# Layer 0 of a two-layer attention kernel: another order of the filler units, the row sums and the normalisation

## The chip, the cores and the metric

The kernel runs on one core of a Trainium2 chip. The metric is the device time of one execution in microseconds (us). Before the change three runs gave a median of 2808.86 us, the lowest 2808.78 and the highest 2810.7. Everything is fp32.

A core has a matrix engine (TensorE, "PE" in the profile, with its weight loads shown apart as "PEld"), a vector engine (VectorE, "DVE"), an engine for functions such as the exponential (ScalarE, "ACT"), a general engine (GpSimd, "POOL") and SyncE ("SP"), which here only issues transfers. Each engine runs its own instructions in its own order and waits at semaphores for the others. Matrix products land in PSUM, which has few buffers; all else lies in SBUF.

## The reference, cut to what matters

The input x has two images of 512 channels and 64x32 = 2048 tokens. Layer 0 is softmax attention with 8 heads of 64. The queries and keys see 64 more channels, 32 that depend on the row (frequency) alone and 32 that depend on the column (time) alone.

```python
emb = get_embeddings(B, H, W, FREQ_DIM, TIME_DIM, dtype)   # (B, 64, H, W): freq[h] and time[w]
qk_hs = concatenate([hidden_states, emb], axis=1)           # reshaped to (B, S, 576)
q = qk_hs @ Wq;  k = qk_hs @ Wk;  v = v_hs @ Wv             # 8 heads of 64
attn = softmax(q @ k^T * scale)
o = (attn @ v) @ Wout + bout
x = o + hidden_states                                       # layer 0

t = tokens(x)
t = t + attention_1(layernorm(t))                           # layer 1: Nystrom attention
t = t + ffn_1(layernorm(t))                                 # weights from 4-bit codes (qidx, scales)
```

The change leaves layer 1 as it is. Of layer 1, only the first layer norm and the preparation of the 4-bit weights are computed while layer 0 runs.

## The kernel before, in words

Layer 0 makes eight passes: two images b times four pairs of heads hp. `attention0` is one pass. It goes over 4 blocks t of 512 tokens and, within a block, over 16 chunks c of 128 keys, two chunks (a *group*) at a time, so 8 groups for a block and 32 for a pass. In the text, (t, c) names a group by its block and its last chunk. For each group the program issues, in this order:

1. the scores of the group (L1040, four 64x64 matmuls for each chunk into a PSUM bank pair), and their exponentials on ScalarE (L1048) into `p_f`, of which there are six buffers, that is three groups;
2. the additions of `p_f` into `acc_f` on VectorE (L1058), which make the softmax denominators;
3. the values of the group before (L1070), into two PSUM banks over the whole block; at the end of a block they are added by ScalarE and VectorE (L1076, L1077);
4. some *filler units*, see below;
5. one step of the preparation of layer 1's weights (`feed_forward_map`, VectorE almost alone, L1135, L1136, L1141), called `beside`, in the groups 1, 3 and 5 of each 8;
6. if a block has just ended, its row sums (`sums`): a matmul with ones (rs_f, L1084), the reciprocal on VectorE (L1088) and the product with the output on GpSimd (L1089).

The filler units keep TensorE busy and prepare the next pass. `Heads0.units` of the next pass gives 15: the query embedding (matmul L863 into fp, copy L865 to the factors `ft`, addition of the row and the column factor to a 128x2048 tile `e` on GpSimd, L867), four query projections (L879, a bank pp, with the addition of `e` on VectorE, L882), the same for the keys, four value projections (vp, L924), and a reduction of the largest entries (L912). Where an image is complete, `finish0_units` joins them: for each block the output projection in four units (yp, L939, with bias and x added on VectorE, L946; the sum x1 is written to DRAM by GpSimd's queue, L982) and the layer norm in steps (`statistics` and `norm0_steps`: L957 to L974, L991 to L995).

Units are Python generators. `advance(gens, n)` takes the first generator that can go on and draws units from it until n are made; a generator that yields GAP steps aside for the next one. How many are drawn in a group follows from `due`, the share of units that should be done by then. In most passes two units are drawn once two are due. While an image is being finished (`every`), one or two units are drawn in each group, and the weight preparation rests.

All of fp, pp, vp, yp, the row sums, and the mean and variance banks take turns in two PSUM buffers (`bank`).

At the start of the kernel, the units of the first pass run with nothing beside them: x, Wq and the embedding arrive, then the queries, keys and values of the first two heads are projected.

Of the kernel before, what the change touches and what calls it, by code (L numbers as in the profile page):

```python
# [19 lines left out]
KC = C // P  # L20
HEADS, D = 8, 64
NPAIR = HEADS // 2
TB = 512
# [638 lines left out]
def fast_path(  # L662
# [62 lines left out]
    def chunked(ap):  # L725
        return ap.rearrange("(k p) n -> p k n", p=P)
# [74 lines left out]


    emb_sb = wpool0.tile([64, H + W], F32, name="emb_f")
    nc.vector.memset(emb_sb, 0.0)
    w_sb = {kind: wpool0.tile([P, KC, C], F32, name=f"w{kind}_f") for kind in "qk"}
    we = {kind: wpool0.tile([64, C], F32, name=f"we{kind}_f") for kind in "qk"}

    def load_w0(kind, cols, queue=nc.sync):
        w = {"q": wq0, "k": wk0}[kind]
        nc.sync.dma_start(w_sb[kind][:, :, cols], chunked(w[:C, cols]))  # L810
        queue.dma_start(we[kind][:, cols], w[C:, cols])

    nc.gpsimd.dma_start(emb_sb[:32, :H], freq)
    nc.gpsimd.dma_start(emb_sb[32:, H:], time)
    load_w0("q", slice(0, P), nc.scalar)

    def load_x(src, b, name, first=0, n=NTB):
        tiles = []
# [21 lines left out]
    class Heads0:  # L840
# [13 lines left out]
        def embedded_and_projected(self, kind):  # L854

            cols, xbs = self.cols, self.xbs
            if kind == "q":
                self.q = qopool.tile([P, S], F32, tag="qo", name=f"q_{self.name}")

            def embedded(kind):  # L860

                fp = bank(f"fp_{kind}_{self.name}")
                nc.tensor.matmul(fp[:, : H + W], lhsT=we[kind][:, cols], rhs=emb_sb, start=True, stop=True)  # L863
                ft = wpool0.tile([P, H + W], F32, tag="ft", name=f"ft_{kind}_{self.name}", bufs=2)
                nc.vector.tensor_copy(ft, fp[:, : H + W])  # L865
                e = wpool0.tile([P, H, W], F32, tag="e", name=f"e_{kind}_{self.name}")
                nc.gpsimd.tensor_tensor(  # L867
                    e,
                    ft[:, :H].unsqueeze(2).to_broadcast([P, H, W]),
                    ft[:, H:].unsqueeze(1).to_broadcast([P, H, W]),  # L870
                    ALU.add,
                )
                return e.rearrange("p h w -> p (h w)")

            def project(kind, dst, e, t):
                toks = slice(t * TB, (t + 1) * TB)
                pp = bank(f"pp_{kind}_{self.name}_{t}")
                for k in range(KC):
                    nc.tensor.matmul(  # L879
                        pp, lhsT=w_sb[kind][:, k, cols], rhs=xbs[t][:, k, :], start=k == 0, stop=k == KC - 1  # L880
                    )
                nc.vector.tensor_tensor(dst[:, toks], pp, e[:, toks], ALU.add)  # L882

            dst = self.q if kind == "q" else self.k
            e = embedded(kind)
            yield
            yield GAP
            for t in range(NTB):
                project(kind, dst, e, t)
                yield  # L890
# [104 lines left out]
        nc.gpsimd.dma_start(chunked(xh_d[b])[:, :, toks], xn)  # L995
        yield

    N_FINISH0 = NTB * (KC + 2)

    def finish0_units(b, oTs, outs_done):  # L1000
        last = None
        for t in range(NTB):
            xb = block_of(lpool, "xr", f"xr_f0_{b}_{t}")
            nc.sync.dma_start(xb, chunked(x[b])[:, :, t * TB : (t + 1) * TB])
            yield from gap()

            for m, _ in enumerate(out0_units(b, t, xb, oTs)):
                if last and m == 0:
                    next(last)
                yield  # L1010
            if t == NTB - 1:
                outs_done.append(True)
            if last:
                yield from gap()
            xn = block_of(lpool, "xn", f"xn_f0_{b}_{t}")
            last = norm0_steps(b, t, xb, xn, xn[:, :2, :])
            next(last)
            yield from gap(2)
            next(last)
            yield  # L1020
            yield from gap(2)
            next(last)
            yield from gap(2)
            next(last)
            yield
        next(last)

    def attention0(hd, filler, n_filler, needed, beside=None, every=False):


        steps = [(t, c) for t in range(NTB) for c in range(NST)]
        av, acc, first, late = None, None, None, None

        def scores(t, c):
            sc = scores_bank(f"sc_{hd.name}_{t}_{c}")
            for r in range(2):
                for h in range(2):
                    rows = slice(h * D, (h + 1) * D)
                    lo = c * P + r * D
                    nc.tensor.matmul(  # L1040
                        sc[r * D : (r + 1) * D, h, :],
                        lhsT=hd.k[rows, lo : lo + D],
                        rhs=hd.q[rows, t * TB : (t + 1) * TB],
                        start=True,
                        stop=True,
                    )
            p = exps(f"p_{hd.name}_{t}_{c}")
            nc.scalar.activation(p, sc, AF.Exp, scale=D**-0.5)  # L1048
            return p

        def add(step, p):
            nonlocal acc, first
            t, c = step
            if c == 0:
                first = p
                acc = apool.tile([P, 2, TB], F32, tag="acc", name=f"acc_{hd.name}_{t}")
            else:
                nc.vector.tensor_tensor(acc, first if c == 1 else acc, p, ALU.add)  # L1058

        def values(step, pp, its_acc):  # L1060

            nonlocal av, late
            t, c = step
            if c == 0:
                av = [values_bank(f"av_{hd.name}_{t}_{r}") for r in range(2)]
            for r in range(2):
                keys = slice(r * D, (r + 1) * D)
                for h in range(2):
                    half = slice(h * D, (h + 1) * D)
                    nc.tensor.matmul(  # L1070
                        av[r][half, :], lhsT=hd.v[keys, c, half], rhs=pp[keys, h, :],
                        start=c == 0, stop=c == NST - 1,
                    )
            if c == NST - 1:
                o = hd.q[:, t * TB : (t + 1) * TB]
                nc.scalar.copy(o, av[0])  # L1076
                nc.vector.tensor_tensor(o, av[1], o, ALU.add)  # L1077
                late = t, its_acc

        def sums(t, acc):  # L1080
            o = hd.q[:, t * TB : (t + 1) * TB]
            rs = bank(f"rs_{hd.name}_{t}")
            for h in range(2):
                nc.tensor.matmul(  # L1084
                    rs[h * D : (h + 1) * D, :], lhsT=ones, rhs=acc[:, h, :], start=True, stop=True
                )
            rinv = row_of(f"rinv_{hd.name}_{t}")
            nc.vector.reciprocal(rinv, rs)  # L1088
            nc.gpsimd.tensor_tensor(o, o, rinv, ALU.mult)  # L1089

        pending, done = [], 0
        for i in range(0, len(steps) + 1, GROUP):
            group = [(step, scores(*step)) for step in steps[i : i + GROUP]]
            for step, p in group:
                add(step, p)
            for step, p, its_acc in pending:
                values(step, p, its_acc)
            pending = [(step, p, acc) for step, p in group]
            due = n_filler * (i + GROUP) // len(steps)
            if every:  # L1100
                done += advance(filler, 2 if due - done >= 2 else 1)
            elif due - done >= 2:
                done += advance(filler, min(due - done, 3))
            if beside and i // GROUP % 8 in (1, 3, 5):
                advance(beside)
            if not group:
                while needed in filler:
                    advance(filler)
            if late:
                sums(*late)  # L1110
                late = None

    def feed_forward_map():

# [559 lines left out]
    cur = Heads0(0, 0, xbs)  # L1674
    drain(cur.units())
    ffn_map = [feed_forward_map()]
    oTs, finish, work = [], None, []
    for n, (b, hp) in enumerate(todo[:-1]):
        nb, nhp = todo[n + 1]
        if nb != b:  # L1680
# [5 lines left out]
        else:  # L1686

            units = nxt.units(False, lambda: outs_done)
            work.append(finish)
            n_fill += N_FINISH0  # L1690
        work.append(units)
        attention0(cur, work, n_fill, units, ffn_map if finish is None else None, finish is not None)
        finish = None
        oTs.append(cur.q)
        if n == 3:
            while ffn_map:
# [3 lines left out]
        if hp == NPAIR - 1:  # L1700
            outs_done = []
            finish = finish0_units(b, oTs, outs_done)
            oTs = []
        cur = nxt
    only0.close()


# [407 lines left out]
```

## Time and profile before

| what | value |
|---|---|
| median of three runs | 2808.86 us |
| the profiled execution, its own time | 2808.29 us |
| its span in the profile | 2806.2 us |
| matmuls busy | 2745.0 us, 98% |
| VectorE busy | 1778.3 us, 63% |
| ScalarE busy | 913.5 us, 33% |
| GpSimd busy | 231.7 us, 8% |
| scores of layer 0 (L1040), busy | 491.7 us, 4096 matmuls |
| values of layer 0 (L1070), busy | 484.3 us, 4096 matmuls |
| query projections of layer 0 (L879) | 117.5 us, 256 matmuls |
| output projections of layer 0 (L939) | 115.9 us, 256 matmuls |
| row-sum reciprocals (L1088) | 107.2 us, 32, 3350 ns each |

The profiled execution took 0.6 us less than the median, and 2.1 us of it lie outside the span. In the rows of groups, the numbers after the bar are the busy time in us, the mean duration of one instruction in ns, and then the idle time of that engine just before, with what ended most of it. An fp32 matmul leaves two records in the timeline, each with its own start. Starts are exact, ends of pipelined matmuls are modelled, so the time from start to start is what a matmul costs when the engine is busy.

### The profile page before, as it was taken

What the parts mean: (1) busy time and instruction counts of PE and PEld (TensorE: products, weight loads), DVE (VectorE), ACT (ScalarE), POOL (GpSimd) and SP (SyncE); (2) the same over time, 40 slices, a digit from 0 to 9 for tenths busy, and PEclk for the clock granted to TensorE, in tenths of its full rate; (3) what the DMA queues carried; (4) which work ended last, traced back from release to release, by engine and by line L of the source; (5) the groups of instructions that cost most, each with busy time, mean ns of one, the idle gap of its engine ahead of it and who ended that gap; (6) DMA issues with size and microseconds to landing.
All of it is one profiled execution on the core that took longest, in us unless ns stands there. A gap on an engine that the chain in (4) does not pass through costs nothing. (4 is left out here: it accounts for less than half of the span.)

```text
span 2806.2 us, 39647 instructions
## 1 busy us (share of the span) xinstructions
PE 2745.0 (98%) x16746; PEld 1374.3 (49%) x16746; DVE 1778.3 (63%) x2109; ACT 913.5 (33%) x1352; POOL 231.7 (8%) x130
## 2 busy tenths in 40 slices
PE   9999999999999999999999999999999999999899
PEld 5343443434343334343344455777667666554333
DVE  2868788784658775767767544545755655556565
ACT  1434343433334334434422223223332323222110
POOL 1101101010101210100002000000100100000000
PEclk9999999999999999999999999999999999999999
DMA  3000000101001200002025632203001102010201
GB/s 113 5 5 1 5 1 1 61 16 46 27 32 60 75 1 1 1 31 67 16 83 180 202 120 89 97 28 114 27 28 50 65 1 86 23 61 19 101 16 46
DMA packets 85626, 140.31 MB, mean 50 GB/s; under 512 B 7856, under 2 KB 42944, under 8 KB 82880
## 3 DMA queue, kind: packets, MB, share of 16 engines
q1 hardware_dynamic: 80944, 120.87, 12.8%
q0 software_dynamic: 4416, 16.79, 1.6%
q8 instruction: 133, 2.18, 0.3%
q14 instruction: 53, 0.43, 0.0%
q10 hardware_dynamic: 80, 0.03, 0.0%
HBM read 82.48 MB, written 55.19 MB: 49 GB/s over the span
## 5 line engine op out<-in xcount | busy, mean ns | idle before, releaser
L1058 DVE TENSOR_TENSOR acc_f<-acc_f,p_f 128x1024 f32<-128x1024 f32 x448 | 611.4, 1365 | 217.8 <-ACT p_f L1048 188.8
L1048 ACT ACTIVATE p_f<-sc_f 128x1024 f32<-128x1024 f32 x512 | 496.8, 1022 | 580.2 <-PE sc_f L1040 574.1
L1040 PE MATMUL sc_f<-q_f,k_f 64*64 64x512 f32 x4096 | 491.7, 595 | 2.9 <-ACT p_f L1048 2.9
L1070 PE MATMUL av_f<-p_f,v_f 64*64 64x512 f32 x4096 | 484.3, 589 | 0.0
L1070 PEld LDWEIGHTS av_f<-p_f,v_f 64*64 64x64 f32 x4096 | 156.5, 133 | 283.0 <-issue 283.0
L1040 PEld LDWEIGHTS sc_f<-q_f,k_f 64*64 64x64 f32 x4096 | 144.8, 133 | 293.8 <-issue 253.0
L1214 PE MATMUL pp<-xh,w 128*128 128x512 f32 x512 | 231.2, 604 | 4.6 <-ACT X L1261 3.9
L1214 PEld LDWEIGHTS pp<-xh,w 128*128 128x128 f32 x512 | 95.7, 192 | 125.8 <-issue 113.9
L1506 PE MATMUL pb<-R 128*128 128x192 f32 (+1 forms) x640 | 149.6, 380 | 1.0 <-DVE M L1519 1.0
L1506 PE MATMUL pa<-M 128*128 128x192 f32 (+1 forms) x640 | 150.6, 380 | 0.0
L1595 DVE RECIPROCAL acc<-acc 128x256 f32<-128x256 f32 x64 | 111.4, 1746 | 46.7 <-ACT acc L1590 46.7
L1089 POOL TENSOR_TENSOR q_f<-q_f,rinv_f 128x512 f32<-128x512 f32 x32 | 68.3, 2135 | 825.6 <-DVE rinv_f L1088 825.5
L1601 POOL TENSOR_TENSOR o<-o,acc 128x512 f32<-128x512 f32 x32 | 53.8, 1682 | 885.1 <-DVE acc L1600 778.1
L924 PE MATMUL vp<-w,xh 128*128 128x128 f32 x1024 | 122.3, 278 | 0.0
L924 PEld LDWEIGHTS vp<-w,xh 128*128 128x128 f32 x1024 | 118.6, 194 | 7.2 <-issue 4.2
L924 PEld LDWEIGHTS vp_f<-wv_f,x 128*128 128x128 f32 x1024 | 115.6, 192 | 12.7 <-issue 11.0
L879 PE MATMUL pp_q_f<-x,wq_f 128*128 128x512 f32 x256 | 117.5, 612 | 4.2 <-DVE q_f L882 3.1
L939 PE MATMUL yp_f<-q_f,wo_f 128*128 128x512 f32 x256 | 115.9, 606 | 4.2 <-DVE rinv_f L1088 3.3
L924 PE MATMUL vp_f<-wv_f,x 128*128 128x128 f32 x1024 | 118.5, 276 | 0.0
L1506 PEld LDWEIGHTS pb<-R 128*128 128x128 f32 x640 | 106.5, 190 | 24.4 <-DVE M L1519 2.1
L1506 PEld LDWEIGHTS pa<-M 128*128 128x128 f32 x640 | 108.2, 193 | 20.4 <-ACT M L1497 2.5
L1654 PE MATMUL fp_g<-xn_g,mT 128*128 128x512 f32 x256 | 115.1, 598 | 0.7 <-ACT p L1568 0.7
(202 smaller groups left out, 3009.6 us busy)
## 6 DMA issues: line engine op xcount, KB each, us to landing
xh<-xh_fd SPq DMA_DIRECT2D x12, 1024.0 KB, 5.4
xr_f<-in_x_dram SPq DMA_DIRECT2D x8, 1024.0 KB, 5.1
x_fd<-xr_f POOLq DMA_DIRECT2D x8, 1024.0 KB, 4.7
xh_fd<-xn_f POOLq DMA_DIRECT2D x8, 1024.0 KB, 4.6
k_fd<-k SPq DMA_DIRECT2D x32, 256.0 KB, 2.7
q_fd<-q SPq DMA_DIRECT2D x32, 256.0 KB, 3.0
xb_g<-x_fd SPq DMA_DIRECT2D x32, 256.0 KB, 4.5
k<-k_fd SPq DMA_DIRECT2D x8, 1024.0 KB, 5.9
```

What stands on the lines that cost most here:

```text
L879: nc.tensor.matmul(pp, lhsT=w_sb[kind][:, k, cols], rhs=xbs[t][:, k, :], start=k == 0, stop=k == KC - 1)
L924: nc.tensor.matmul(vp[:, j * P : (j + 1) * P], lhsT=xb[:, k, j * P : (j + 1) * P], rhs=w_of(k), start=k == 0, stop=k == KC - 1,)
L939: nc.tensor.matmul(yp, lhsT=wo_sb[:, k, m * P : (m + 1) * P], rhs=oTs[k][:, toks], start=k == 0, stop=k == NPAIR - 1,)
L1040: nc.tensor.matmul(sc[r * D : (r + 1) * D, h, :], lhsT=hd.k[rows, lo : lo + D], rhs=hd.q[rows, t * TB : (t + 1) * TB], start=True, stop=True,)
L1048: nc.scalar.activation(p, sc, AF.Exp, scale=D**-0.5)
L1058: nc.vector.tensor_tensor(acc, first if c == 1 else acc, p, ALU.add)
L1070: nc.tensor.matmul(av[r][half, :], lhsT=hd.v[keys, c, half], rhs=pp[keys, h, :], start=c == 0, stop=c == NST - 1,)
L1089: nc.gpsimd.tensor_tensor(o, o, rinv, ALU.mult)
L1214: nc.tensor.matmul(pp, lhsT=self.w[j][:, c, :], rhs=xhs[t][:, c, :], start=c == 0, stop=c == KC - 1)
L1506: nc.tensor.matmul(dst, lhsT=lhsT[:, k, t * P : (t + 1) * P], rhs=rhs[:, k, :], start=k == 0, stop=k == 1)
L1595: nc.vector.reciprocal(half, half)
L1654: nc.tensor.matmul(fp, lhsT=mT[:, k, m * P : (m + 1) * P], rhs=self.xn[:, k, :], start=k == 0, stop=k == KC - 1,)
```

## The change

It has five parts.

- **Order of finishing an image.** `finish0_units` now only does the output projections of all four blocks, with the next block's x loaded ahead into the other of two buffers, and writes x1 to DRAM. A new generator, `norm0_units`, waits until that is done, then reads x1 back from DRAM block by block and makes the normalisation in steps. It takes the place of `beside` in the passes of the second image.
- **Drawing of units.** `every` is gone. In all passes four units are drawn, once four are due. `beside` is advanced in every second group, not in three of eight.
- **Row sums.** `sums` of a block is called one group later than before, except at the end of a pass.
- **First embedding sums.** For the first pass alone, the two additions that make `e` are done by VectorE, not by GpSimd.
- **Queues at the start.** The two embedding loads move from GpSimd's queue to ScalarE's, behind the first slice of Wq, which moves there from SyncE's; the memset of the embedding tile is split in two halves, so that it does not overlap the loaded parts.

```diff
-    nc.vector.memset(emb_sb, 0.0)
+    nc.vector.memset(emb_sb[:32, H:], 0.0)
+    nc.vector.memset(emb_sb[32:, :H], 0.0)
...
     def load_w0(kind, cols, queue=nc.sync):
         w = {"q": wq0, "k": wk0}[kind]
-        nc.sync.dma_start(w_sb[kind][:, :, cols], chunked(w[:C, cols]))
+        queue.dma_start(w_sb[kind][:, :, cols], chunked(w[:C, cols]))
         queue.dma_start(we[kind][:, cols], w[C:, cols])
 
-    nc.gpsimd.dma_start(emb_sb[:32, :H], freq)
-    nc.gpsimd.dma_start(emb_sb[32:, H:], time)
     load_w0("q", slice(0, P), nc.scalar)
+    nc.scalar.dma_start(emb_sb[:32, :H], freq)
+    nc.scalar.dma_start(emb_sb[32:, H:], time)
...
-                nc.gpsimd.tensor_tensor(
+
+                engine = nc.gpsimd if self.b or self.hp else nc.vector
+                engine.tensor_tensor(
...
     def finish0_units(b, oTs, outs_done):
...
+        def load(t):
+            xb = block_of(lpool, ("xr", "xn")[t % 2], f"xr_f0_{b}_{t}")
+            nc.sync.dma_start(xb, chunked(x[b])[:, :, t * TB : (t + 1) * TB])
+            return xb
+
+        nxt = load(0)
+        yield from gap()
         for t in range(NTB):
...
+            xb = nxt
+            if t + 1 < NTB:
+                nxt = load(t + 1)
+            yield from out0_units(b, t, xb, oTs)
+        outs_done.append(True)
+
+    def norm0_units(b, outs_done):
+
+        while not outs_done:
+            yield
+        for t in range(NTB):
+            xb = block_of(lpool, "xr", f"x1_f0_{b}_{t}")
+            nc.sync.dma_start(xb, chunked(x1_d[b])[:, :, t * TB : (t + 1) * TB])
+            yield
+            xn = block_of(lpool, "xn", f"xn_f0_{b}_{t}")
+            for _ in norm0_steps(b, t, xb, xn, xn[:, :2, :]):
                 yield
...
-            if every:
-                done += advance(filler, 2 if due - done >= 2 else 1)
-            elif due - done >= 2:
-                done += advance(filler, min(due - done, 3))
-            if beside and i // GROUP % 8 in (1, 3, 5):
+            if due - done >= 4:
+                done += advance(filler, 4)
+            if beside and i // GROUP % 2:
                 advance(beside)
             if not group:
                 while needed in filler:
                     advance(filler)
-            if late:
-                sums(*late)
-                late = None
+                ended = late
+
+            if ended:
+                sums(*ended)
+            ended, late = late, None
...
-        attention0(cur, work, n_fill, units, ffn_map if finish is None else None, finish is not None)
+        attention0(cur, work, n_fill, units, norm if b else ffn_map)
...
             finish = finish0_units(b, oTs, outs_done)
+            next(finish)
+            norm.append(norm0_units(b, outs_done))
```

By the order of instructions, a pass that prepares weights now has the query embedding's factors at (1,1), the row sums of block 0 at (1,3), the four query projections at (1,5), the keys' factors at (2,7), the four key projections at (2,11) and the four values at (3,11). Before, they went in pairs at (0,9) to (3,11), and the row sums of block 0 stood at (1,1). The first pass of the second image has the output projections of the four blocks at (0,9), (1,1), (1,9) and (2,1).

## The prediction, made before the changed kernel was run

> **What bounds the kernel now.** I read the busy shares first, then the waits of TensorE, then the stages that those point to. The change touches layer 0 alone (up to about 1421 us of the span).
>
> ```profile
> span 2806.2 us, 39647 instructions
> PE 2745.0 (98%) x16746; PEld 1374.3 (49%) x16746; DVE 1778.3 (63%) x2109; ACT 913.5 (33%) x1352; POOL 231.7 (8%) x130
> ...
> L1058 DVE TENSOR_TENSOR acc_f<-acc_f,p_f 128x1024 f32<-128x1024 f32 x448 | 611.4, 1365 | 217.8 <-ACT p_f L1048 188.8
> ```
>
> TensorE is 98% busy, so a gain must come from its few waits or from busy time that isn't arithmetic. VectorE looks idle for a third of the time, but its sums line waits for the exponentials 188.8 of 217.8 idle us. It follows at short distance in the first five passes, where it also prepares the weights of layer 1.
>
> ```profile
> PE rs_f L1084 <- DVE acc_f L1058: 3.8, 4, 1.2
> PE yp_f L939 <- DVE rinv_f L1088: 3.3, 2, 2.4
> PE pp_q_f L879 <- DVE q_f L882: 3.1, 1, 3.1
> PE sc_f L1040 <- ACT p_f L1048: 2.9, 8, 0.9
> PE mean_n L961 <- DVE xn_f L958: 2.8, 1, 2.8
> ...
> PE var_n L974 <- DVE xr_f L971: 1.6, 1, 1.6
> ```
>
> Columns: us in all, times, longest. All are stalls in layer 0 by VectorE (one by ScalarE). The head, in windows (us; busy PE, PEld, DVE, ACT, POOL; clock):
>
> ```profile
> 16.00:19.40 3.40, 0.28 (x2) 0.04 (x1) 0.79 (x2) 0.00 (x0) 2.58 (x1) 1.00 1.09 356
> 19.40:28.20 8.80, 8.80 (x17) 3.58 (x17) 1.19 (x2) 0.00 (x0) 0.00 (x0) 0.81 0.81 230
> ```
>
> and in the timeline, with the place in the second pass where a first query projection is put among the attention:
>
> ```profile
> 14.96 3.62 POOL L867 TENSOR_TENSOR e_q_f<-ft_q_f 128x2048 f32<-128x2048 f32 x1 [11.54 <-issue]
> 19.36 8.83 PE L879 MATMUL pp_q_f<-x,wq_f 128*128 128x512 f32 x16 [3.12 <-DVE q_f L882]
> ...
> 239.74 1.90 PE L1070 MATMUL av_f<-p_f,v_f 64*64 64x512 f32 x16
> 241.56 7.13 PE L879 MATMUL pp_q_f<-x,wq_f 128*128 128x512 f32 x16
> 241.72 5.80 DVE L1058 TENSOR_TENSOR acc_f<-acc_f,p_f 128x1024 f32<-128x1024 f32 x2
> 241.93 4.51 POOL L867 TENSOR_TENSOR e_q_f<-ft_q_f 128x2048 f32<-128x2048 f32 x1 [13.51 <-DVE ft_q_f L865]
> 248.63 1.95 PE L1040 MATMUL sc_f<-q_f,k_f 64*64 64x512 f32 x16
> 249.56 2.55 DVE L1058 TENSOR_TENSOR acc_f<-acc_f,p_f 128x1024 f32<-128x1024 f32 x2
> 250.40 1.90 PE L1070 MATMUL av_f<-p_f,v_f 64*64 64x512 f32 x16
> 252.11 1.90 PE L1040 MATMUL sc_f<-q_f,k_f 64*64 64x512 f32 x16
> ```
>
> Two things to see. First, sixteen attention records take 252.11-250.40 = 1.71 us from start to start, but 241.56-239.74 = 1.82 before the projection and 250.40-248.63 = 1.77 after it, and the projection takes 7.07 for 6.86 (16 records of 0.429). So one **excursion** from 64x64 tiles to another form and back costs about 0.36 us (0.11+0.20+0.05). Second, a pair of sums takes 2.55 us, and 5.80 while GpSimd adds an embedding.
>
> [...] the trace has half-clock windows of 3.413 us starting at 20.44, 727.0 and 942.0, each soon after a stall of 2.4 to 3.1 us. [...] here one sum goes from 1.22 to about 4.5 us.
>
> **The change, part by part (time of TensorE, start to start).** Matched against ideal pitches, TensorE loses 31.8 us in layer 0, besides the drains.
>
> *Four units at once, projections first: excursions.* By the two programs' order on TensorE, layer 0 makes 105 excursions before and 73 after. 32 x 0.36 = **-11.5**. The matmuls are the same.
>
> *First embedding on VectorE, its loads on another queue: head.* The first query projection starts at 9.11 and its four units end at 28.12: 19.01 for 32 matmuls of two records, 32 x 0.429 = 13.73; 5.3 lost (3.1 wait, 2.2 half clock). GpSimd starts the embedding at 14.96 although the factors are ready at 9.47. On VectorE, with 2.28 us (the 128x2048 subtraction of L962), it is done at about 11.8. The x blocks land at 12.3, 15.0, 17.8, when they are needed or before; the ScalarE queue has no other work then. **-5.2**.
>
> *Row sums a group later.* The 32 rs_f matmuls wait 4.95 us by pitches for the last addition of VectorE (3.8 in the waits view, the rest are shorter). With 3.43 us more of scores and values before them nearly all goes: **-4.9**. Reciprocal and GpSimd product come later, and their result is read a pass later.
>
> *Output projections first, normalisation from DRAM.* The stretch 721 to 972 us loses 14.2 us: yp waits for the reciprocal and for additions, mean and var wait, and two half-clock windows of 1.7 us each. After, yp come by fours with x loaded ahead, norm steps lie 8.6 us or more apart (one each second group), so that each matmul finds its input: **-14.2**, and a 0.9 us wait at 564.7 goes: **-0.9**. The norm re-reads 4 x 1 MB from DRAM; the same transfer (in_x) lands in 5.1 us, and a step of 6.9 us lies between. On SP these four loads stand behind loads of x that don't wait; nothing urgent follows. Square root and the exponential's table (0.69 + 1.28 us) fit before the next exponential.
>
> Sum of gains: 11.5+5.2+4.9+14.2+0.9 = **36.7 us**.
>
> *What four units at once cost.* All these units use one PSUM tag of two buffers, shared with the row sums. Before, two units found both free. After, in a pass with weight preparation, the order is: factor fp_q in group (1,1) (block, last chunk), row sums 0 in (1,3), four query units in (1,5). The second unit takes the buffer of row sums 0, thus waits for the reciprocal (3.27 us pitch), which stands on VectorE behind all sums of (1,3). And VectorE does more: weight preparation steps (2.1 us: two hits pairs of 0.42+0.69) in 4 of 8 groups rather than 3.
>
> I made a ledger for the second pass, in us from its first score (217.96), VectorE's instructions by their own durations: first addition ends 9.4 (as now, behind a reciprocal of the pass before, 222.87 to 226.2), then sums end at (0,3) 12.8, (0,5) 17.5, (0,7) 20.0, (0,11) 27.1, (0,15) 34.2, each followed by 2.1 for a hits step every second group; (1,1) 37.5, output sum 0.6, factors 0.2; GpSimd's embedding then makes (1,3) end at 44.0 instead of 40.8; 1.3 for scales; reciprocal to 48.6. TensorE: scores of (1,3) at 30.3, row sums at 34.3, (1,5) at 35.3, the batch starts at 38.9; the first unit ends at 42.5, the second waits until 48.7: 6.2 lost. Its own eviction and the row sum add 0.6 and 0.35: **7.2 us**, and a half-clock window of 1.7.
>
> The same working gives 2.5 for the first pass, 6.6 for the third, 0 for the fourth (weight preparation has other steps there), 0 for the fifth, 4.3 for the sixth (mean 2.0 and its start 1.4), 2.8 for the seventh: 7.2+2.5+6.6+4.3+2.8 = **+23.4**; three half-clock windows **+5.1**. ScalarE's exponentials need the sums of three groups before (six p_f buffers); that bears a lag of some 9 us, which isn't reached. Bounds: if VectorE recovers some 6 us more than I reckon, 0 to 5; if each stall is 3 us longer, 45.
>
> Net -36.7+28.5 = -8.2: 2808.3-8.2 = 2800.1 against the profiled execution, which is 0.6 below the median and 2.1 above its span. Forecast 2800.
>
> **Rivals.**
> (B) *The stall of the batch doesn't come* because VectorE is close behind the exponentials at (1,3). For it: now it catches up in every block, and the sums take 1.22 us alone. Against it: the 5.80 pair. Then 2808.3-36.7+5 = 2777.
> (C) *Slower: VectorE also holds up the key batches.* At (2,11) four key units stand in one group, their embedding asked of GpSimd two groups before. By the ledger this batch has 0.8 us to spare. Every weight or norm step that VectorE does late, and every sum stretched to 4.5 us by GpSimd, goes into a wait of TensorE there and at (1,5). More than 13.8 us beyond my 28.5, 2.3 in each of six passes, makes the kernel measurably slower; at 3.2 in each it is 2808.3-36.7+28.5+19 = 2819. [...] Against: later passes have no weight preparation.
> (D) *The excursions are not the price of a change of tile form*, but of something that stays per unit: 2808.3-25.2+28.5 = 2811.6.
>
> **How the numbers follow.** 0.2% (5.6 us) is about what a measurement of this kernel can tell from no change: faster is below 2803.2, slower above 2814.5. The ledger (own range 2794 to 2806) has 0.48: 0.34 faster, 0.14 same. B 0.17: faster. C 0.25: 0.05 same, 0.20 slower. D 0.10: 0.02 faster, 0.06 same, 0.02 slower. In all 0.53, 0.25, 0.22. The range 2781 to 2817 leaves out about a tenth at each end: half of B below, the worse half of C above.
>
> **What would show it.** Right: TensorE's records dense from 9 to 28 us; no waits of rs_f for acc_f above 0.3; none of yp_f for rinv_f; a wait of pp_q_f for the reciprocal of about 6 us in the second and third pass; 73 excursions at 0.36. Wrong: pp_k_f waits of over 2 us in each pass (C); no pp_q_f wait (B); attention groups above 3.43 us without a wait named, or exponentials waiting for acc_f (then the lag is larger than the buffers bear); waits of mean or var for the re-read x1.

## The result and the profile after

The changed kernel takes 2827.02 us (median of four runs, 2825.05 to 2830.39) where the kernel before took 2808.82 (2808.51 to 2810.7) beside it: a ratio of 1.0068, 95% interval 1.0053 to 1.0083. It is 18.2 us slower, where 8.8 us less were forecast. The profiled execution has a span of 2826.5 us, 20.3 more than before.

The page of the changed kernel, with the lines that answer to those of before (lines from L867 on have moved by 2 or 3):

```profile
span 2826.5 us, 39665 instructions
## 1 busy us (share of the span) xinstructions
PE 2754.9 (97%) x16746; PEld 1380.4 (49%) x16746; DVE 1787.4 (63%) x2112; ACT 915.5 (32%) x1354; POOL 223.5 (8%) x126
...
L1060 DVE TENSOR_TENSOR acc_f<-acc_f,p_f 128x1024 f32<-128x1024 f32 x448 | 607.0, 1355 | 173.6 <-ACT p_f L1050 139.5
...
L1072 PE MATMUL av_f<-p_f,v_f 64*64 64x512 f32 x4096 | 499.8, 595 | 19.9 <-DVE q_f L1079 19.9
```

VectorE's sums take about the same time (607.0 us, 611.4 before), but they wait 139.5 us for the exponentials where they waited 188.8: VectorE is late more often. The last line is new. In the kernel before, the values waited for nothing at all (the last number below); now they wait 19.9 us.

```profile
L1070 PE MATMUL av_f<-p_f,v_f 64*64 64x512 f32 x4096 | 484.3, 589 | 0.0
```

The waits of TensorE in layer 0 after the change (us in all, times, longest), with those of layer 1 left out:

```profile
PE av_f L1072 <- DVE q_f L1079: 19.9, 6, 5.4
...
PE sc_f L1042 <- ACT p_f L1050: 4.9, 11, 0.9
...
PE pp_q_f L882 <- DVE rinv_f L1090: 1.1, 1, 1.1
```

The waits of the row sums for `acc_f` are gone, and of the 3.3 us that yp waited for the reciprocal 0.9 are left. The wait of 6 to 7 us that the prediction put at the query batch is only 1.1. One stands instead that it did not name: the first values of a block wait for L1079, VectorE's addition of the two `av` banks of the block before. Those two banks have one buffer each. The timeline of the second pass, at the start of its block 1:

```profile
245.10 5.21 DVE L1060 TENSOR_TENSOR acc_f<-acc_f,p_f 128x1024 f32<-128x1024 f32 x4
...
247.76 1.03 PE L1072 MATMUL av_f<-p_f,v_f 64*64 64x512 f32 x4
...
252.35 1.22 DVE L1060 TENSOR_TENSOR acc_f<-p_f,p_f 128x1024 f32<-128x1024 f32 x1
...
253.48 0.68 DVE L1079 TENSOR_TENSOR q_f<-av_f,q_f 128x512 f32<-128x512 f32 x1
...
254.22 3.68 PE L1072 MATMUL av_f<-p_f,v_f 64*64 64x512 f32 x12 [5.42 <-DVE q_f L1079]
```

At 247.76 TensorE begins the values of block 1: four records, which go to the bank that ScalarE has already copied. The other twelve wait for the end of L1079 at 254.16. VectorE is then still busy with sums of block 0, does a weight step (L1137, L1138) between 250.2 and 252.4 and then the first sum of block 1; L1079 stands behind them all. The same place in windows (columns as before; the clock is the third number from the end):

```profile
230.00:247.70 17.70, 17.70 (x166) 6.31 (x160) 16.78 (x19) 10.27 (x12) 0.00 (x0) 1.00 0.01 2
247.70:251.30 3.60, 1.09 (x8) 0.15 (x2) 3.41 (x5) 1.39 (x2) 0.00 (x0) 1.00 0.00 0
251.30:261.50 10.20, 7.28 (x26) 1.62 (x29) 10.06 (x17) 0.00 (x0) 4.48 (x1) 0.50 0.00 0
```

In the first window VectorE is busy 16.78 of 17.70 us: a long stretch of attention without a projection between. In the third the clock is 0.50 for 10.2 us, of which the first 2.9 still lie inside the wait: TensorE is busy 7.28 us there. In the kernel before, the records of a query projection start 0.429 us apart at 1.00 and 0.853 at 0.50 (24.16 to 27.60 us and 21.05 to 23.61), so half of the time at 0.50 is reckoned as lost. The stall thus costs twice: the wait of 5.42 us, and half of some 7.3 us. By the records of the clock layer 0 has 41.0 us at half clock after the change and 10.2 before. Half of that is 20.5 and 5.1 us; TensorE stood idle in 4.4 of the 41.0, so 18.3 are lost after the change.

Where the 20.3 us of span come from: apart from drains, TensorE loses 64.0 us in layer 0 by starts, 31.8 before, which is +32.2. The span without this loss is 2762.5 instead of 2774.4: -11.9, the excursions saved. The sum is +20.3. (Of the 11.9, 1.0 lies behind layer 0, which ends 21.2 us later than before; 10.9 are left for the excursions.) Of the 32.2, 12.0 are waits that the view names in layer 0 (32.0 against 20.0) and some 13 are half clock; the rest are losses by starts that no wait names.

### The profile page after: what moved, and what is told of

Its sections match the earlier page's. It is cut to its first block, busy times and chain, and to the rows that moved or that the text cites. A ratio compares the mean times of both kernels' runs of the same rounds, so it can differ in the third digit from the quotient of the medians.

```text
span 2826.5 us, 39665 instructions
## 1 busy us (share of the span) xinstructions
PE 2754.9 (97%) x16746; PEld 1380.4 (49%) x16746; DVE 1787.4 (63%) x2112; ACT 915.5 (32%) x1354; POOL 223.5 (8%) x126
## 3 DMA queue, kind: packets, MB, share of 16 engines
q0 software_dynamic: 4352, 16.78, 1.6%
## 5 line engine op out<-in xcount | busy, mean ns | idle before, releaser
L1060 DVE TENSOR_TENSOR acc_f<-acc_f,p_f 128x1024 f32<-128x1024 f32 x448 | 607.0, 1355 | 173.6 <-ACT p_f L1050 139.5
L1072 PE MATMUL av_f<-p_f,v_f 64*64 64x512 f32 x4096 | 499.8, 595 | 19.9 <-DVE q_f L1079 19.9
L942 PE MATMUL yp_g<-o,wo_f 128*128 128x512 f32 x256 | 114.5, 596 | 0.0
```

The source lines that it names most:

```text
L942: nc.tensor.matmul(yp, lhsT=wo_sb[:, k, m * P : (m + 1) * P], rhs=oTs[k][:, toks], start=k == 0, stop=k == NPAIR - 1,)
L1072: nc.tensor.matmul(av[r][half, :], lhsT=hd.v[keys, c, half], rhs=pp[keys, h, :], start=c == 0, stop=c == NST - 1,)
```

## The experiments

The theories, with letters of their own, apart from those of the prediction's rivals. A (block start): between batches of four, VectorE gets a dozen groups of attention in a row; it comes late to L1079, and the values wait. B: VectorE's load alone, a step in 4 groups of 8 rather than 3. C: the late row sums. E, added later: the batches of four by themselves. Each kernel was timed in five rounds beside the kernel before.

**One part undone at a time.** Two units drawn instead of four:

```diff
-            if due - done >= 4:
-                done += advance(filler, 4)
+            if due - done >= 2:
+                done += advance(filler, min(due - done, 3))
```

> The changed kernel, but two units are drawn once two are due, as before the change. Theory A (block start): the first values of a block wait for VectorE's addition of the block before (L1079), which empties the single PSUM bank av, because between batches of four units VectorE gets a dozen groups of attention in a row and falls behind; units in between give it time. Expects the waits of av_f for q_f to fall from 19.9 to under 4 us, half-clock time in layer 0 from 41 us (20.5 lost) to under 15, 94 instead of 73 excursions (21 x 0.36 = 7.6 us back): 2795 to 2806 us. Rival B (VectorE's load alone: a weight or norm step in 4 of 8 groups instead of 3): the waits stay over 12 us, 2818 us or more. Rival C (row sums a group later): waits and time about as in the changed kernel, 2827.

A step in three groups of eight:

```diff
-            if beside and i // GROUP % 2:
+            if beside and i // GROUP % 8 in (1, 3, 5):
```

> The changed kernel, but a weight or norm step only in groups 1, 3 and 5 of 8, as before the change. A step is 2.1 us of VectorE. Theory A: each block start comes 2.1 us less late; waits of av_f for q_f 8 to 14 us (from 19.9), 2810 to 2822 us. Rival B (the load of VectorE is the cause, the batches are harmless): the waits vanish (under 3 us), 2795 to 2803 us. Rival C: 2827.

The row sums at once:

```diff
-                ended = late
-            if ended:
-                sums(*ended)
-            ended, late = late, None
+            if late:
+                sums(*late)
+                late = None
```

> The changed kernel, but the row sums of a block are put in at once, not a group later. Theory A: the addition L1079 stands ahead of the reciprocal in both orders; TensorE now waits at the row sums (rs_f for acc_f, 8 us or more) for a part of what it waited for at av_f; the sum of both is as before, time within 6 us of 2827. Rival C (the late row sums are the cause): waits of av_f gone and no new ones, 2800 to 2812 us. Rival B: 2827.

Measured: two_units 2825.69 us (ratio to before 1.0066, 1.0052 to 1.0079), three_of_eight 2817.94 (1.0036, 1.0024 to 1.0048), sums_at_once 2810.15 (1.0006, 0.9998 to 1.0015). A's expectation holds for the second kernel alone. Undoing the batches brought 1.3 us, not 21 to 32, and the av waits were still 13.2 us, as B had it; but in the second kernel, where B expected waits under 3 us, they are 12.2. Undoing the row sums brought 16.9 us although A said it would bring at most 6; the time is C's, but not the waits, for rs_f now waits 13.4 us for `acc_f`. No theory of one cause stands. Therefore the parts were also undone in combination:

> The changed kernel with two units at once and a weight or norm step in 3 of 8 groups, both as before the change; row sums stay a group later. Theory A, widened by the runs so far (what counts is how late VectorE is when a block begins: steps, places of the units and order of the sums add up, and none alone explains it): VectorE is no later than in the kernel before, so the waits of av_f for q_f are under 4 us, half-clock loss in layer 0 under 7 us, and the gains of the other parts show: 2808.5-4.3 (head, as measured) -14 (finish) -3 (row sums) -5 (91 excursions against 105) = 2782; 2780 to 2792. Rival C (late row sums cost by themselves, since the values that wait stand before them): waits of av_f over 8 us, 2798 us or more.

> The changed kernel with a weight or norm step in 3 of 8 groups and the row sums at once, both as before the change; four units at once stay. The single edits gave 2817.9 and 2810.2 against 2827.0. Theory A: both shorten the same lateness, so the gains overlap in part: 2798 to 2806 us, waits of rs_f and av_f together 5 to 10 us. Rival B (steps and order are separate costs that add): 2827-9-17 = 2801 or less, waits under 4 us. Rival E (the batches of four are the cause by themselves): 2808 us or more.

> The changed kernel with two units at once, 3 of 8 steps and row sums at once, all as before the change: what stays of it is the order of finishing (projections first, norm from DRAM) and the start. Theory A: no lateness beyond that of the kernel before: 2808.5-4.3-14 = 2790; 2786 to 2796 us, 105 excursions, rs_f waits for acc_f again 3 to 6 us. If the new order of finishing costs by itself (the norm steps load VectorE in the sixth and seventh pass): 2797 us or more, with waits of av_f, rs_f or mean_n over 4 us there.

Together (medians; "4/8" is a step in four groups of eight; excursions by the order of the instructions; the last column is half of the time at half clock in layer 0, from the clock records, of which up to 2.2 us fell on an idle TensorE):

| parts of the change present | us | excursions | half of half clock, us |
|---|---|---|---|
| none of the three (all_three_back) | 2801.6 | 105 | 0 |
| late sums (two_and_three) | 2801.1 | 91 | 1.7 |
| four units (three_at_once) | 2807.9 | 76 | 11.9 |
| four units, 4/8 (sums_at_once) | 2810.2 | 72 | 13.7 |
| four units, late sums (three_of_eight) | 2817.9 | 77 | 10.2 |
| 4/8, late sums (two_units) | 2825.7 | 94 | 11.9 |
| all three (the changed kernel) | 2827.0 | 73 | 20.5 |

two_and_three has the small waits and the small clock loss that A expected, but its time is 9 us above A's range, and all_three_back is 6 us above, where the second reading in its expectation (the new finishing costs by itself, 2797 us or more) holds; the finishing, which both have, is taken up below. three_at_once is 2 us above A's range, with waits of rs_f for acc_f of 17.7 us, which is nearer to E. Read row by row: late sums alone cost nothing (-0.5). Four units alone cost 6.3, although 29 excursions of 0.36 us are saved. Late sums cost 10.0 on top of four units (known to some 4 us only, since the six runs of three_of_eight spread from 2812.3 to 2821.0), and 16.9 on top of four units and 4/8. 4/8 costs 24.6 on top of late sums, with no batches of four, and 2.3 with four units and the sums at once. What costs most is the late sums together with a late VectorE; the batches aren't needed for it.

One part alone in the kernel before:

```diff
-            if beside and i // GROUP % 8 in (1, 3, 5):
+            if beside and i // GROUP % 2:
```

> The kernel before with one part of the change alone: a weight step in 4 of 8 groups instead of 3 (its own row sums, units in pairs, finishing and start). Theory A: VectorE needs 2.55+1.05+0.4 us for a group of 3.43 and comes late at the block starts: rs_f waits for acc_f and av_f waits for q_f go from 3.8 to over 12 us, half clock follows, 2818 us or more. Rival E (only the batches of four make VectorE late): 2808 to 2812 us.

Measured 2811.73 (1.0015, 1.0009 to 1.0022): 4.1 us slower, not 10, and in the range of E, which two_units contradicts. This run and two_units have the same units at the same places in the first pass and the same load of VectorE; there they differ in the late sums, and in the start before the pass. The output sum of block 1 (L1079, L1077) begins 78.4 us after the first scores of the pass in the one and 78.3 in the other, so VectorE is equally late. It shows what the late sums do. The timelines at the start of block 2 of the first pass, first of two_units, then of before_four_of_eight, each with a window of the 6.8 us after it:

```profile
130.59 1.03 PE L1072 MATMUL av_f<-p_f,v_f 64*64 64x512 f32 x4
...
133.15 0.68 DVE L1079 TENSOR_TENSOR q_f<-av_f,q_f 128x512 f32<-128x512 f32 x1
...
133.89 2.83 PE L1072 MATMUL av_f<-p_f,v_f 64*64 64x512 f32 x10 [2.26 <-DVE q_f L1079]
```

```profile
133.90:140.70 6.80, 6.80 (x16) 2.27 (x17) 2.29 (x2) 0.00 (x0) 0.00 (x0) 0.50 0.01 2
```

```profile
132.33 1.08 PE L1084 MATMUL rs_f<-acc_f,ones 128*64 128x512 f32 x4 [0.97 <-DVE acc_f L1058]
...
133.34 1.95 PE L1040 MATMUL sc_f<-q_f,k_f 64*64 64x512 f32 x16
...
135.45 0.68 DVE L1077 TENSOR_TENSOR q_f<-av_f,q_f 128x512 f32<-128x512 f32 x1
```

```profile
136.20:143.00 6.80, 6.80 (x24) 2.79 (x25) 6.70 (x4) 0.23 (x1) 2.12 (x1) 1.00 0.01 2
```

With the row sums at once, TensorE waits 0.97 us for the last sum, does row sums and scores, and by then most of VectorE's lateness has passed; the values lose about 1.1 us more by starts. With late sums, the row sums stand behind the values that wait. All the lateness falls on one wait of 2.26 us, and behind it the clock is 0.50 for 6.8 us; in the other kernel it stays 1.00 (what decides this is taken up in the last section).

**The bank taken out.** ScalarE copies both banks, VectorE adds the copies:

```diff
                 nc.scalar.copy(o, av[0])
-                nc.vector.tensor_tensor(o, av[1], o, ALU.add)
+                half = apool.tile([P, TB], F32, tag="rinv", name=f"oh_{hd.name}_{t}")
+                nc.scalar.copy(half, av[1])
+                nc.vector.tensor_tensor(o, half, o, ALU.add)
```

> The changed kernel, but ScalarE copies both av banks to SBUF (0.59 us more a block), and VectorE adds the two copies there, so that TensorE's bank does not wait for VectorE. VectorE's work is the same. Theory A: the waits of av_f for q_f go (under 1 us for ScalarE's copy), 19.9 us and their half clock; but VectorE is as late as before, so the next wait is the one that the prediction named: the second of four query units waits for the reciprocal of the row sums, 6 to 7 us in the second and third pass and some 5 in the passes with norm steps: 2808 to 2822 us. Rival D (the lag itself isn't that large; only the single bank makes it cost): no new wait over 2 us, 2790 to 2800 us.

Measured 2815.77 (1.0025, 1.0015 to 1.0035). The waits view of act_copy has no line of av_f for q_f any more; it begins with

```profile
PE pp_q_f L882 <- DVE rinv_f L1092: 16.0, 5, 6.0
```

A's expectation holds in time, and nearly in waits. This is the wait that the prediction reckoned with, at the place and of the size it named (6.0 us the longest). It was hidden behind an earlier one: a VectorE that comes late is met first by the values, and when these have waited, the batch finds it in time.

**Start and finishing.** The kernel before with the new start alone (the edits to the loads, the memsets and the engine of `e`, as in the change):

> The kernel before with the start of the changed one alone: the first two embedding additions on VectorE and the loads on ScalarE's queue. In the changed kernel's profile the first scores start 4.3 us earlier (52.85 against 57.19). If nothing gives that back: 2808.5-4.3 = 2804.2, 2802.5 to 2805.5 us, and the first scores at about 53. If it is only a shift within other waits: 2807 to 2810.

Measured 2803.43 (0.9984, 0.9977 to 0.9990), 4.5 us faster, as expected. all_three_back (2801.59; 0.9979, 0.9971 to 0.9987) has the new finishing besides. That brings 1.8 us more, not 14, and the two intervals overlap. The waits of TensorE in head_only,

```profile
PE rs_f L1086 <- DVE acc_f L1060: 4.2, 4, 1.5
...
PE yp_f L941 <- DVE rinv_f L1090: 3.3, 2, 2.4
...
PE sc_f L1042 <- ACT p_f L1050: 2.9, 8, 0.9
PE mean_n L963 <- DVE xn_f L960: 2.8, 1, 2.8
...
PE var_n L976 <- DVE xr_f L973: 1.6, 1, 1.6
```

and in all_three_back:

```profile
PE rs_f L1086 <- DVE acc_f L1060: 9.6, 8, 1.6
PE sc_f L1042 <- ACT p_f L1050: 7.8, 15, 1.6
...
PE yp_f L942 <- DVE rinv_f L1090: 0.9, 1, 0.9
```

The waits for mean and variance are gone, and most of those of yp. Row sums and scores wait more instead, 10.3 us together: the normalisation now lies in passes full of attention and makes VectorE late there. The timeline of all_three_back, at such a place:

```profile
947.87 3.34 POOL L996 TENSOR_TENSOR xn_f<-xn_f,rstd_n 128x1024 f32<-128x1024 f32 x1 [5.81 <-DVE rstd_n L994]
...
948.92 7.37 DVE L1060 TENSOR_TENSOR acc_f<-acc_f,p_f 128x1024 f32<-128x1024 f32 x4
...
952.38 1.02 ACT L1050 ACTIVATE p_f<-sc_f 128x1024 f32<-128x1024 f32 x1 [5.08 <-DVE acc_f L1060]
...
953.46 1.09 PE L1042 MATMUL sc_f<-q_f,k_f 64*64 64x512 f32 x8 [1.61 <-ACT p_f L1050]
```

Four sums take 7.37 us, with GpSimd multiplying in the first 2.29 of them; four without it took 5.21 (at 245.10 in the changed kernel). The exponentials wait for a free `p_f` buffer, and the scores for them. From the first scores of the fifth pass to those of the eighth it takes 558.4 us in head_only and 559.2 in all_three_back: the fifth pass is 17.0 us shorter, the sixth and seventh together are 17.8 longer.

**VectorE's steps moved under the batches.** If lateness is the cause, the same steps cost nothing while TensorE is busy with a batch:

```diff
-        pending, done = [], 0
+        pending, done, credit = [], 0, 0
...
             if due - done >= 4:
-                done += advance(filler, 4)
-            if beside and i // GROUP % 2:
-                advance(beside)
+                for _ in range(4):
+                    if not advance(filler):
+                        break
+                    done += 1
+                    if not hd.b:
+                        advance(beside)
+                    else:
+                        credit = 3
+            if hd.b and credit:
+                advance(beside)
+                credit -= 1
```

> The changed kernel (four units at once, row sums a group later, the same finishing), but a weight step follows each unit of a batch instead of every second group, and norm steps stand in the three groups from a batch on. VectorE does the same work; it does the steps while TensorE is busy with a batch of 13.7 us, not in the stretches of attention alone, where a group gives it 3.43 us for 2.55 of sums and 2.1 of a step. Theory A (VectorE's lateness at a block's start is the whole cause): no wait of av_f for q_f over 2 us in the passes with weight steps, half-clock loss in layer 0 under 7 us, and the excursions saved (74 against 105, 11.2 us) show: 2808-4.5 (start)-11-5 (row sums)-2 (finish, as measured) = 2785; 2780 to 2792 us. If the batches or the late sums stall by themselves, av_f or pp_q_f waits stay over 10 us and the time is 2800 us or more.

Measured 2797.91 (0.9965, 0.9952 to 0.9979), the lowest median of the study: 29 us less than the changed kernel with four units, late sums and the same finishing. No wait of av_f for q_f is left. From the first scores of the first pass to those of the fifth it takes 652.5 us; 660.5 before, 675.8 in the changed kernel. The named waits at the query batch in pass 2 and 3 are 0.7 us each. A lighter load of VectorE isn't the reason: the additions of L1138 are 17, 21 and 18 in the first three passes, 20, 22 and 14 in the changed kernel, and three_of_eight with 14, 17, 17 and 8 in four passes took 2817.9 us. It missed its range by 6 us; in the second image, where the norm steps follow the batches, passes five to seven take 564.0 us, 560.3 before.

Two attempts at this rest failed. The copies of act_copy put on top:

> As steps_in_batches, and ScalarE copies both av banks to SBUF, so that TensorE's bank doesn't wait for VectorE at all. Theory A: where VectorE is in time the bank costs nothing, so this is within 3 us of steps_in_batches, 2778 to 2792 us. If a lateness remains in the passes with norm steps, the wait moves from av_f to pp_q_f or sc_f, and the time still differs by under 5 us.

Measured 2803.15 (0.9984, 0.9977 to 0.9991), some 5 us slower than without the copies, more than its expectation allowed: they gain nothing where VectorE is in time, scores wait 8.1 us for exponentials instead of 5.8, and by the clock records up to 3.4 us more are lost. And the norm steps of the fifth pass back in every second group:

```diff
-            if hd.b and credit:
+            if hd.b and (credit if hd.hp else i // GROUP % 2):
```

> As steps_in_batches, but in the first pass of the second image the norm steps stand in every second group again, as in the changed kernel; in the two passes after it they stand behind the batches. In steps_in_batches that first pass lost some 11 us at its end (the query batch behind norm steps of VectorE and GpSimd 7.5, mean, variance and row sums the rest), in the changed kernel almost nothing there. Theory A: these go for the larger part and nothing new comes: 6 to 11 us less than steps_in_batches (2797.9), 2787 to 2792 us. If the lateness only moves to the next pass: within 3 us of it.

Measured 2799.08 (0.9970, 0.9961 to 0.9980), the same, as the second reading of its expectation had it. The loss at the end of the fifth pass went and came back in the sixth and seventh (one wait of rs_f for acc_f of 6.3 us at the end of the sixth, with half clock behind it). The lateness was moved, not removed.

## Why the prediction was wrong

TensorE's losses in layer 0 were to grow by 3.3 us (28.5 less the 25.2 of gains beside the excursions) and grew by 32.2. The step that failed is the path of TensorE in the ledger: it took VectorE's lateness to be met first by the query batch, and passed over the values of the block, which meet it before and wait 19.9 us in six places. With that the late row sums, put down as a gain of 4.9, became a loss. Two terms were mis-sized besides: the finishing and the clock.

**Excursions, -11.5: right, as far as the matching of starts shows it.** The part of the span that isn't loss fell by 11.9 us, 10.9 of it in layer 0. No run tested this term alone; rival D, which had none of it, has nothing to set against the fall.

**Start, -5.2: right.** head_only measured -4.5, with an interval of -2.8 to -6.5, and in its profile the first scores begin 5.3 us earlier. In the changed kernel they begin 4.3 us earlier; a first block of x lands late for 0.5 us in the one and 1.4 in the other.

**Row sums, -4.9: the waits went, but the place was mispriced.** "With 3.43 us more of scores and values before them nearly all goes" is true of the row sums. That a late VectorE would then be met by the values themselves, in one piece, was not seen; taken back alone, the late sums are worth 16.9 us of loss in the changed kernel.

**Finishing, -14.2: wrong.** That stretch lost most of its waits as said, but "norm steps lie 8.6 us or more apart (one each second group), so that each matmul finds its input" looked at the norm's own matmuls alone. VectorE's work stayed and now delays sums in other passes. By the medians 1.8 us of the gain are left; the intervals of head_only and all_three_back overlap, so even this isn't shown.

**Four units at once, +28.5: the step that decided.** The ledger of VectorE was right to 0.4 us: it has the output sum end at 38.1 us after the first score of the pass, and in the changed kernel L1079 ends at 254.16-215.69 = 38.5. But TensorE's side of the ledger goes from "scores of (1,3) at 30.3" straight to "row sums at 34.3" and steps over the values between them, at 30.3+1.7 = 32.0. These need the bank that L1079 empties, and so wait 38.1-32.0 = 6.1 by the ledger's own numbers (5.42 measured). The prediction asked which wait holds the batch and only followed the PSUM tag of the units; the one-buffer `av` banks, filled by other lines, were not on its list. act_copy shows that the mechanism it did name exists, as the second in line; the same lateness stands behind both, which is why the 23.4 us of waits reckoned are near the 21.0 measured at the values and the batch. And two_units has 13.2 us of waits at the values with units in pairs: the step in four groups of eight, counted under this head, and the late sums bring them, not the batches.

**The clock, +5.1: mis-sized.** Three half-clock windows were reckoned with; layer 0 has 41.0 us of half clock, twelve windows of 3.41, which cost 18.3 us. With one stall of 5.42 us came 10.2 us of half clock, three windows and not one.

The prediction's rival C ended near the measured time (2819) by luck, for a reason that did not hold: key batches wait 1.2 us in all. Its general point, that VectorE's lateness turns into waits of TensorE at other places than reckoned, was the right one.

What stays open: what brings a second and third window at half clock. 4/8 was not run alone on the base of all_three_back, only in the kernel before. Why the copies cost some 5 us in steps_in_batches was not followed further than the waits named.

## What to carry to other kernels

When fewer, larger batches of filler save changes of tile form (32 fewer here; the time of layer 0 that isn't loss fell by 10.9 us), the engine that used the gaps between them must be reckoned anew: list every buffer that it empties, the one-deep ones first, and find the first instruction in the bound engine's order that needs one. Put side work on that engine under the batches, not between them; here this paid for the weight steps (652.5 us for the first four passes, 675.8 in the changed kernel), and for the norm steps it did not (564.0 for passes five to seven, 560.3 before). And look for what a late engine meets first: with other work put between, the same lateness cost less here (waits of 0.97 and about 1.1 us at full clock, against 2.26 us and 6.8 us at half clock behind it).

## What the runs showed of the hardware

Half clock made some waits of TensorE much dearer than they are long. In the first pass, lateness met as one wait of 2.26 us was followed by 6.8 us at 0.50; the same lateness met as waits of 0.97 and about 1.1 us with 2.7 us of matmuls between left it at 1.00. Around the wait of 5.42 us, 10.2 us ran at 0.50, 7.3 of them behind it, which took some 3.7 us more.

In the traces of the kernels before and after, the eight stretches of half clock in layer 0 were 3.41 us long (three), 6.83 (three) or 10.24 (two), and within each trace their starts lie a whole number of times 3.413 us apart. Divided by this step, each trace shows the half clock go with the idle time of TensorE (by the modelled ends) in the one step before it: that was 2.33 to 2.68 us before the change and 2.08 to 3.41 after, and no step at full clock with 1.64 us or less was followed by one. So in these traces it is not the length of a wait alone that counts, but how much of it falls into one step. A later wait of two_units shows it:

```profile
264.55 1.93 PE L1072 MATMUL av_f<-p_f,v_f 64*64 64x512 f32 x12 [2.46 <-DVE q_f L1079]
```

It is longer than the 2.26 us, but by the same step, counted from the half clock that began at 133.90, an edge lies at 263.60 (38 steps on) and splits it into 1.51 and 0.95 us. The twelve records behind it take 1.93 us, where the twelve at 254.22 in the changed kernel took 3.68 at 0.50: the clock was not halved. Some of the differences in clock between the kernels above may therefore be a matter of where their waits fall on this grid.
